# Order of the background work in a selective-scan layer: when y is written back, how the first image is normed, how the last image is finished

## Chip, cores and metric

The kernel runs on one core of a Trainium2 chip. It is one program that computes four layers one after the other. The metric is device time in microseconds (us); the time of a kernel is the median of several runs. The engines are TensorE (PE in the profile), VectorE (DVE), ScalarE (ACT), GpSimd (POOL) and SyncE (SP, which here issues DMAs only). Each engine runs its own instructions strictly in order.

## The reference, cut to what matters

The input x is 8 images of 64 channels of 64 x 64 points. Layer 0 holds the whole change; its middle part is this (C = 64, DI = 128, N = 16, four scan directions):

```python
def _selective_scan(xs, dts, A, Bs, Cs, D):     # per direction k, channel d, state n
    def step(h, inp):
        u_t, dt_t, B_t, C_t = inp
        h = h * exp(dt_t[..., None] * A) + dt_t[..., None] * B_t[:, :, None, :] * u_t[..., None]
        return h, einsum('bkcn,bkn->bkc', h, C_t)
    ...
    return ys + D * xs

def _ss2d(x, ...):                              # x is already layer-normed over the channels
    xz = einsum('bhwc,dc->bhwd', x, in_proj_w) + in_proj_b
    xi, z = split(xz, 2)
    xc = silu(dwconv3(xi, conv_w, conv_b))      # 3 x 3, per channel
    xs = [rows of xc, columns of xc, rows reversed, columns reversed]
    dts, Bs, Cs = split(einsum('bkdl,kcd->bkcl', xs, xproj_w), [R, R + N])
    dts = softplus(einsum('bkrl,kdr->bkdl', dts, dtproj_w) + dtproj_b)
    out_y = _selective_scan(xs, dts, A, Bs, Cs, Ds)
    y = sum of the four directions, each put back into the order of the image
    y = ln(y, outnorm_g, outnorm_b) * silu(z)
    return einsum('bhwd,cd->bhwc', y, outproj_w) + outproj_b

xh = x + _ss2d(ln(x, ln1_g, ln1_b), ...)
return xh + _safm(channel_ln(xh), ...)
```

What follows (`_safm`, a layer with channel and spatial attention, one with an inner optimisation, one with attention) is the same before and after the change. It starts by reading `xh`, two images at a time.

## The kernel before, in words

`scan_layer` (L203 to L743) computes `xh`. An image is held with its 128 inner channels on the partitions and its 4096 points along the free axis. Points are cut twice: into 8 *blocks* of 512 (`BK`[...]) for everything around the scan, and into 4 *chunks* of 1024 (`CH`) for the scan itself.

**Steps and units.** A *step* is one direction k on one chunk c; an image has 16 steps (L643: directions in the order 0, 2, 1, 3, that is rows, rows reversed, columns, columns reversed; reversed directions take the chunks from the last to the first). A step has 16 *units*, one for each state n. Eight images give 128 steps and 2048 units. A unit n (`unit`, L585) does this:

- VectorE multiplies B, broadcast to all partitions (`bt`), by `du` = dt * u, into PSUM (`bdu`, L594). For n = 3 and 8 (`BY_POOL`) GpSimd does this product ahead of time and in place (`product`, L583), from a copy of the same numbers in SBUF (`dus`).
- VectorE runs the scan h = a * h + bdu along the 1024 points (L598).
- ScalarE copies the last column of h to `state`, from which the next chunk starts (L602).
- GpSimd multiplies the broadcast C (`ct`) by h, in place (L607). The multiplies of the units before n = 3 and n = 8 are held back by one unit, so that GpSimd does unit 3's own before unit 2's, and 8's before 7's.

Two units later `sum_up` (L621) has TensorE add the product into the PSUM tile `yps` by a matmul with the identity (L636). The tile begins, at n = 0 of a step, with the skip term (direction 0, weight `skipd`, source u) or with the y of the directions before (identity, source y; both L631). After n = 15 it is complete, and `empty` (L612) has ScalarE copy it to `y` (L616). There is one buffer of `yps`: the next step's L631 waits for that copy. `empty` is called at the head of each `sum_up`.

**What a unit needs and when it is issued.** The loop in L706 to L734 issues, around `unit(ctl, n)`: the load of `bt` for unit n + 3 and of `ct` for unit n + 1 (`load`, L566; on SP's queue, from a DRAM scratch `bc`; 4 buffers of `bt`, 5 of `ct`, so that a load waits on the queue until a buffer is free, and what is behind it on the queue waits too); `decay` for unit n + 2, on ScalarE (a = exp(A_n dt), L575, 3 buffers); `product` for n + 2. Past n = 15 these are those of the next step. The next step's `du` is copied by ScalarE into PSUM inside unit 15, between its product and its scan (`place_input`, L550), since there is one buffer of `du`.

**The background.** Everything else is cut into *items*, pairs of a `make` (mostly a matmul into one of two PSUM banks, tag "mm") and a `use` (mostly an activation that empties it). `Background` (L165) keeps them in a queue. In each unit, `bg.before()` ahead of the unit's own work makes the next item, and `bg.after()` behind it issues the DMAs that the item before left (`later`), then the `use` of the previous unit's item. So there is one item in a unit. Items are:

- `project` (L476), for the next step, put at the head of the queue: B and C (`lower`, twice; ScalarE copies to `e`, then a DMA to `bc`), dt before softplus (`step_size`, twice), softplus in three parts (Abs, Exp; Ln, Relu on ScalarE; a sum on GpSimd, `soft3`), and for columns one copy that turns u (`turn`). `soft3` and `step_input` (the `dus` product on GpSimd) are issued behind units 8 and 11, behind unit 13 in the first image's first four steps.
- `before` (L352), for the next image: 8 loads of x, `norm_items` (L271), 8 `project_in` into the padded image `pad`, 8 `gate` (z = Silu, stored to DRAM `zd`), 8 `convolve` (nine taps by nine matmuls with diagonal matrices, L405, in four items of 3, 2, 2 and 2 taps, in the first image in two of 5 and 4; then Silu into `u`).
- `after` (L427), for the image before: `norm_items` on y, product with z on GpSimd (`multiply`), `project_out` with the residual, store to `xh`.

`norm_items` is the layer norm for all 8 blocks: `centre` (subtract the mean by a matmul, square), `variance` (a matmul that gives a row, `vrow`, stored to DRAM), `fetch` (all variances back as 128 x 32), `root`, `invert`, store, `back` (1/std as rows), `apply` per block (spread by a matmul, multiply on VectorE, scale and offset on ScalarE).

**The ends.** In the first image there is no image before it to hide its `before`: `start(0)` and a `bg.drain()` run its loads, norm, projections and the first two convolutions ahead of step 0 (L685 to L693); convolutions 2s and 2s + 1 for s = 1 to 3 are put in front of step s's own items and so are done in step s - 1, and the gates follow in step 4. Before the last step of an image the queue is emptied (the `while bg.queue` ahead of `prepare(b + 1, 0)`). After the last step of the last image come the last sums, `empty`, and `after(7)` with nothing beside it. Then the next layer's first load, x (L1154), waits for `xh` of images 0 and 1 and its place in SP's queue, and its norm begins with L136.

## Time and profile before

The median is 13172.89 us of 3 runs (13163.58 to 13174.3). The profiled execution took 13181.03 us; its span, from the first instruction to the last, is 13179.2 us.

| stretch, us from the span's start | what runs | DVE busy | PE busy | ACT busy | POOL busy | PE clock granted |
|---|---|---|---|---|---|---|
| 0 to 123 | ahead of the first scan | 13.57 | 99.06 | 45.65 | 9.12 | 1.00 |
| 123 to 7723 | the 128 steps | 7162.75 | 6059.21 | 4790.90 | 6050.11 | .91 |
| 7723 to 7805 | after the last scan, until the next layer's first matmul on its x | 8.21 | 65.60 | 28.01 | 22.41 | .65 |
| 7805 to 13179 | the three other layers and the rest of layer 0 | 3797.89 | 4903.18 | 2867.00 | 694.68 | .94 |

How to read the lines shown later. A *group* line names line, engine, operation, output <- inputs, shape and count, then the total busy time and the mean of one in ns, then the idle time of the engine just before these instructions and what ended most of it. A line of the view by source line gives min/median/max in ns, then the stretch of the span in which they lie. A line of the *waits* gives the engine and the line that waited, what it waited for, the total, the number of times and the longest, in us. A *timeline* line gives start and duration in us, engine and line, and in square brackets how long the engine had been idle before it and what it waited for; SPq is the DMA queue's issue. Idle time of an engine that is not the one that sets the end costs nothing. The matmuls' ends are modelled.

### The profile page before, as it was taken

To read this page: it belongs to the slowest core of one execution; us is meant where nothing else is said; L and a number is where in the kernel's file an instruction comes from. 1 tells how busy PE (TensorE), PEld (TensorE's weight loads), DVE (VectorE), ACT (ScalarE), POOL (GpSimd) and SP (SyncE) were. 2 spreads that over 40 slices of the span, in tenths; PEclk is the share of its full clock that TensorE was granted. 3 is DMA by queue.
4 is the path that set the end of the run, shared out by engine and by line. 5 is a ranking of instruction groups with operands and counts; after the bars stand their busy time and mean duration, and the time that the engine had idled before them with its cause. 6 is when DMAs were issued, how large, how long until landed. Compare 5 with 4: busy or idle time off the path is not lost. (4 is left out here: it accounts for less than half of the span.)

```text
span 13179.2 us, 115966 instructions
## 1 busy us (share of the span) xinstructions
PE 11127.1 (84%) x36395; PEld 4134.4 (31%) x36395; DVE 10982.4 (83%) x7626; ACT 7731.6 (59%) x10048; POOL 6776.3 (51%) x3126
## 2 busy tenths in 40 slices
PE   8787887788888878877877779999997778999999
PEld 2232232232232232322322223323324554333332
DVE  6999999999999999999999958686686786666666
ACT  5675666665666766665765536455464674544544
POOL 5778878778778778778778840000002772000000
PEclk9898999898999999999998879999998788999999
DMA  5888888888888888888888840000001010000000
GB/s 196 289 281 291 302 290 294 293 286 301 292 285 306 288 291 300 290 285 303 288 287 299 289 158 9 23 13 17 17 6 63 29 37 25 5 17 17 5 11 6
DMA packets 684840, 2333.69 MB, mean 177 GB/s; under 512 B 96784, under 2 KB 97456, under 8 KB 681648
## 3 DMA queue, kind: packets, MB, share of 16 engines
q1 hardware_dynamic: 684208, 2326.13, 51.1%
q8 instruction: 290, 4.75, 0.1%
q14 instruction: 342, 2.80, 0.1%
HBM read 2240.69 MB, written 76.28 MB: 176 GB/s over the span
## 5 line engine op out<-in xcount | busy, mean ns | idle before, releaser
L607 POOL TENSOR_TENSOR ct<-ct,h 128x1024 f32<-128x1024 f32 x2048 | 4820.7, 2369 | 1546.7 <-DVE h L598 779.5
L636 PE MATMUL yps<-ct,ident 128*128 128x512 f32 x8192 | 4157.3, 641 | 542.2 <-POOL ct L607 540.9
L598 DVE TENSOR_TENSOR_SCAN h<-a,state,bdu 128x1024 f32<-128x1024 f32 x1344 | 3153.9, 2347 | 193.1 <-POOL ct L607 15.1
L892 DVE TENSOR_TENSOR sum<-sum,ex 128x1024 f32<-128x1024 f32 x1920 | 2348.0, 1223 | 767.0 <-ACT ex L885 653.6
L885 ACT ACTIVATE ex<-sc 128x1024 f32<-128x1024 f32 x2048 | 1985.1, 1021 | 1526.5 <-PE sc L880 1526.3
L636 PEld LDWEIGHTS yps<-ct,ident 128*128 128x128 f32 x8192 | 1573.6, 202 | 3084.1 <-issue 1893.4
L575 ACT ACTIVATE a<-dt,amat 128x1024 f32<-128x1024 f32 x2048 | 2337.2, 1142 | 22.7 <-POOL dt L528 19.5
L594 DVE TENSOR_TENSOR bdu<-bt,du 128x1024 f32<-128x1024 f32 x1792 | 2194.4, 1225 | 186.7 <-ACT du L554 123.8
L899 PE MATMUL av<-ex,v 128*64 128x512 f32 x8192 | 1985.9, 606 | 0.0
L602 ACT COPY state<-h 128x1 f32<-128x1 f32 x2048 | 381.4, 186 | 2251.4 <-DVE h L598 2247.6
L880 PE MATMUL sc<-q,k 16*128 16x512 f32 (+1 forms) x8192 | 1655.0, 628 | 5.0 <-ACT ex L885 4.4
L598 DVE TENSOR_TENSOR_SCAN h<-a,bdu 128x1024 f32<-128x1024 f32 x448 | 1024.5, 2287 | 65.7 <-ACT state L602 4.8
L899 PEld LDWEIGHTS av<-ex,v 128*64 128x64 f32 x8192 | 497.7, 136 | 1361.6 <-issue 1358.2
L880 PEld LDWEIGHTS sc<-q,k 16*128 16x128 f32 (+1 forms) x8192 | 562.5, 184 | 1078.4 <-ACT ex L885 744.3
L1197 POOL TENSOR_TENSOR gt<-gt,pad 128x1024 f32<-128x1024 f32 x16 | 34.9, 2181 | 1617.6 <-ACT gt L1196 1535.5
L631 PE MATMUL yps<-y,ident 128*128 128x512 f32 x384 | 344.7, 1039 | 386.3 <-ACT y L616 386.3
L583 POOL TENSOR_TENSOR bt<-bt,dus 128x1024 f32<-128x1024 f32 x256 | 603.1, 2356 | 5.2 <-DMA bt<-bc 4.7
L598 DVE TENSOR_TENSOR_SCAN h<-a,state,bt 128x1024 f32<-128x1024 f32 x192 | 566.3, 2950 | 20.5 <-POOL bt L583 19.0
L405 PE MATMUL vps<-pad,convd 128*128 128x512 f32 x1152 | 535.4, 594 | 1.5 <-ACT z L390 1.5
L1570 DVE RECIPROCAL r<-e 128x512 f32<-128x512 f32 x128 | 420.7, 3323 | 0.0
L512 ACT ACTIVATE dt<-tps,dtb 128x512 f32<-128x512 f32 x256 | 175.1, 684 | 361.6 <-PE tps L505 361.6
L528 POOL TENSOR_TENSOR dt<-dt,e 128x1024 f32<-128x1024 f32 x128 | 300.9, 2351 | 111.0 <-ACT dt L525 111.0
(402 smaller groups left out, 10439.3 us busy)
## 6 DMA issues: line engine op xcount, KB each, us to landing
bt<-bc SPq DMA_DIRECT2D x2048, 512.0 KB
ct<-bc SPq DMA_DIRECT2D x2048, 512.0 KB
x<-x SPq DMA_DIRECT2D x12, 2048.0 KB
bc<-e SPq DMA_DIRECT2D x256, 64.0 KB
zd<-z SPq DMA_DIRECT2D x64, 256.0 KB
z<-zd SPq DMA_DIRECT2D x64, 256.0 KB
x<-x SPq DMA_DIRECT2D x32, 512.0 KB
part<-x SPq DMA_DIRECT2D x128, 128.0 KB
```

What stands on the lines that cost most here:

```text
L405: nc.tensor.matmul(held[0].rearrange("p (r c) -> p r c", c=S), convd[:, t, :], pad[:, j * rows + dy : (j + 1) * rows + dy, dx : dx + S], s ...
L575: nc.scalar.activation(ctl["a", n], ctl["dt"], AF.Exp, scale=amat[:, ctl["k"], n : n + 1])
L583: nc.gpsimd.tensor_tensor(bt, bt, ctl["dus"], ALU.mult)
L594: nc.vector.tensor_tensor(z, bt, ctl["du"], ALU.mult)
L598: nc.vector.tensor_tensor_scan(h[:, flip], a[:, flip], z[:, flip], 0.0 if state is None else state[:, n : n + 1], ALU.mult, ALU.add,)
L607: nc.gpsimd.tensor_tensor(ct, ct, h, ALU.mult)
L636: nc.tensor.matmul(ctl["ps"][:, bass.ts(i, BK)], cm.ident, ct[:, bass.ts(i, BK)], start=False, stop=(n == N - 1),)
L880: nc.tensor.matmul(sc[:, e, :], k[r : r + d, bass.ts(j, 128)], qs[i][r : r + d, :], start=True, stop=True,)
L885: nc.scalar.activation(ex, sc, AF.Exp)
L892: nc.vector.tensor_tensor(sums[i], sums[i], ex, ALU.add)
L899: nc.tensor.matmul(avs[i][r, :], v[:, j, r], ex[:, e, :], start=(j == 0), stop=(j == TQ - 1))
L1570: nc.vector.reciprocal(r[n][s], e[n][:, s])
```

## The change

**y is written back sooner.** `empty` leaves `sum_up` and stands at the head of each unit, in front of the background item and the unit's own work. In unit 13 no background item is started (`bg.before(n == N - 3)`), though the `use` of unit 12's still runs. In unit 15 the next step's `decay` is issued behind `unit` (and so behind `place_input`) and not in front of it.

**The first image is normed in three parts.** `norm_items` takes the blocks it is for, and scales its DRAM row and its small tiles to them. For image 0 it is made three times, for blocks 0 to 2, 3 and 4, 5 to 7 (`FIRST`), each followed by the projections of these blocks. The first part and convolutions 0 and 1 stay ahead of step 0; the second goes into step 0, the third into step 1, each in front of the two convolutions that were there before; in step 2 are the last two convolutions. In these three steps (`early`) each unit has three background items, the two more behind it. `pad` is filled to the end two steps later than before.

**The last image ends with rows and is finished beside its last steps.** The directions of image 7 come in the order 1, 3, 0, 2. Direction 2 goes through the chunks from the last to the first, so that after each of its steps two blocks of y are final. `after` takes the blocks it is for; in steps 13, 14 and 15 of image 7 (`late`) it is added behind unit 4 for the two blocks of the step before, and these steps have two items a unit. After the last step only blocks 0 and 1 are left. Because y no longer begins with direction 0, the skip term goes with the first four steps of an image (`new_y`), whichever direction these are. `load` of x and z in `after` becomes one item ahead of the last two `apply`.

For images 1 to 6 the items are the same as before but for one more item in each `after` (the `load`).

```diff
@@ -181,7 +181,7 @@
         self.late.append(do)
 
-    def before(self):
+    def before(self, skip=False):
         self.now = None
-        if self.queue:
+        if self.queue and not skip:
             make, use = self.queue.popleft()
             self.now = (use, make() if make else None)
@@ -269,10 +269,10 @@
             return psum.tile([128, BK], F32, name=name, tag="mm")
 
-        def norm_items(src, dst, p, consts, g, b):
-
+        def norm_items(src, p, consts, g, b, blocks=range(NBK)):
 
             cen, avg = consts
-            var = dr.tile([L], F32, name="vard", tag="vard")
-            rs = dr.tile([L], F32, name="rsd", tag="rsd")
+            j0, nb = blocks[0], len(blocks)
+            var = dr.tile([L], F32, name="vard", tag="vard")[: nb * BK]
+            rs = dr.tile([L], F32, name="rsd", tag="rsd")[: nb * BK]
             sq, sm = {}, {}
 
...
@@ -336,18 +336,21 @@
                 def use(ps):
                     nc.vector.tensor_tensor(src[:, blk], src[:, blk], ps[:p], ALU.mult)
-                    nc.scalar.activation(dst(j), src[:, blk], AF.Identity, bias=b, scale=g)
+                    nc.scalar.activation(src[:, blk], src[:, blk], AF.Identity, bias=b, scale=g)
 
                 return make, use
 
-            out = [centre(0), centre(1)]
-            for j in range(NBK):
+            none = (None, None)
+            out = [centre(j) for j in blocks[:2]]
+            for j in blocks:
                 out.append(variance(j))
-                if j + 2 < NBK:
+                if j + 2 - j0 < nb:
                     out.append(centre(j + 2))
-            none = (None, None)
             out += [none, (None, fetch), none, (None, root), (None, invert), none, (None, back)]
-            out += [none] + [apply(j) for j in range(NBK)]
+            out += [none] + [apply(j) for j in blocks]
             return out
 
+
+        FIRST = (range(3), range(3, 5), range(5, 8))
+
         def before(b):
 
@@ -420,10 +423,11 @@
                 ]
 
-            items = [(None, load(j)) for j in range(NBK)]
-            items += norm_items(xn, lambda j: xn[:, bass.ts(j, BK)], C, ln1, ln1_g, ln1_b)
-            items += [project_in(j) for j in range(NBK)]
+            items = [[(None, load(j)) for j in range(NBK)]]
+            for blocks in (FIRST if b == 0 else (range(NBK),)):
+                items.append(norm_items(xn, C, ln1, ln1_g, ln1_b, blocks))
+                items[-1] += [project_in(j) for j in blocks]
             return u, zd, items, [gate(j) for j in range(NBK)], [convolve(j) for j in range(NBK)]
 
-        def after(b, y, zd):
+        def after(b, y, zd, blocks=range(NBK)):
 
             xf = x_in[b].rearrange("c h w -> c (h w)")
@@ -454,16 +458,19 @@
                     nc.scalar.activation(xo[:C], po[:C], AF.Identity, bias=outb)
                     bg.later(lambda: nc.sync.dma_start(xh[b][:, bass.ts(j, BK)], xo[:C]))
-                    if j + 3 < NBK:
+                    if j + 3 in blocks:
                         load(j + 3)
-                    if j + 2 < NBK:
+                    if j + 2 in blocks:
                         multiply(j + 2)
 
                 return make, use
 
-            items = norm_items(y, lambda j: y[:, bass.ts(j, BK)], DI, lno, on_g, on_b)
-            items[-4] = (items[-4][0], lambda ps, use=items[-4][1]: (use(ps), load(0), load(1)))
-            items[-1] = (items[-1][0], lambda ps, use=items[-1][1]: (use(ps), load(2)))
-            items += [(None, lambda _: (multiply(0), multiply(1))), (None, None)]
-            return items + [project_out(j) for j in range(NBK)]
+            def begin(_):
+                for j in blocks[:2]:
+                    multiply(j)
+
+            items = norm_items(y, DI, lno, on_g, on_b, blocks)
+            items.insert(-2, (None, lambda _: [load(j) for j in blocks[:3]]))
+            items += [(None, begin), (None, None)]
+            return items + [project_out(j) for j in blocks]
 
         def ordered(t, k, c):
@@ -622,9 +629,8 @@
 
 
-            empty()
             ctl, n, ct = pending.popleft()
             if n == 0:
                 ctl["ps"] = psy.tile([DI, CH], F32, name="yps", tag="yps")
-                wt, src = (skipd, ctl["u"]) if ctl["k"] == 0 else (cm.ident, ctl["y"])
+                wt, src = (skipd, ctl["u"]) if ctl["new_y"] else (cm.ident, ctl["y"])
                 so, half = ordered(src, ctl["k"], ctl["c"]), BK // S
                 for i in range(CH // BK):
@@ -641,8 +647,13 @@
                 full.append(ctl)
 
-        steps = []
-        for k in (0, 2, 1, 3):
-            cs = range(NCH) if k < 2 else range(NCH - 1, -1, -1)
-            steps += [(k, c, i) for i, c in enumerate(cs)]
+        def steps(b):
+
+
+            out = []
+            for k in (0, 2, 1, 3) if b < NB - 1 else (1, 3, 0, 2):
+                cs = range(NCH) if k < 2 else range(NCH - 1, -1, -1)
+                out += [(k, c, i) for i, c in enumerate(cs)]
+            return out
+
         images = {}
 
@@ -660,5 +671,5 @@
             return dict(
                 k=k, c=c, u=u, y=y, dt=dt, bc=bc, ut=ut, soft3=soft3, new=new, state=None,
-                first=(i == 0),
+                first=(i == 0), new_y=(s < NCH),
             )
 
@@ -671,9 +682,9 @@
             y = io.tile([DI, L], F32, name="y", tag="y")
             images[b] = (u, zd, y)
-            bg.add(items)
+            bg.add(items[0] + items[1])
             if b == 0:
-                for s in range(1, NCH):
-                    later[s] = convs[2 * s] + convs[2 * s + 1]
                 bg.add(convs[0] + convs[1])
+                for s in range(1, NCH):
+                    later[s] = sum(items[s + 1 : s + 2], []) + convs[2 * s] + convs[2 * s + 1]
                 later[NCH] = gates
             else:
@@ -697,11 +708,12 @@
             place_input(ctl)
             for b in range(NB):
-                for s in range(len(steps)):
-                    if s + 1 < len(steps):
+                for s in range(4 * NCH):
+
+
+                    early, late = b == 0 and s + 1 < NCH, b == NB - 1 and s > 3 * NCH
+                    if s + 1 < 4 * NCH:
                         nxt = prepare(b, s + 1)
                     else:
-                        while bg.queue:
-                            bg.before()
-                            bg.after()
+                        bg.drain()
                         nxt = prepare(b + 1, 0)
 
@@ -713,21 +725,32 @@
 
                     for n in range(N):
-                        bg.before()
+                        empty()
+
+                        bg.before(n == N - 3)
                         ahead(load, n + 3, 0)
                         ahead(load, n + 1, 1)
-                        ahead(decay, n + 2)
+                        if n < N - 1:
+                            ahead(decay, n + 2)
                         ahead(product, n + 2)
                         unit(ctl, n, nxt)
+                        if n == N - 1:
+                            ahead(decay, n + 2)
                         if len(pending) + len(ready) > LAG:
                             sum_up()
                         bg.after()
+                        for _ in range(2 * early + late):
+                            bg.before()
+                            bg.after()
 
-                        if n == (13 if b == 0 and s < NCH else 8) and nxt:
+                        if n == (13 if early else 8) and nxt:
                             nxt["soft3"]()
-                        if n == (13 if b == 0 and s < NCH else 11) and nxt:
+                        if n == (13 if early else 11) and nxt:
                             step_input(nxt)
 
                         if s == 0 and n == LAG + 2 and b > 0:
                             bg.add(after(b - 1, images[b - 1][2], images.pop(b - 1)[1]))
+                        if late and n == LAG + 2:
+                            c = 4 * NCH - s
+                            bg.add(after(b, images[b][2], images[b][1], range(2 * c, 2 * c + 2)))
                         if s == (1 if b else NCH) and n == 0 and b + 1 < NB:
                             bg.add(later.pop(NCH, []))
@@ -740,5 +763,5 @@
                 sum_up()
             empty()
-            bg.add(after(NB - 1, images[NB - 1][2], images[NB - 1][1]))
+            bg.add(after(NB - 1, images[NB - 1][2], images[NB - 1][1], range(2)))
             bg.drain()
 
```

## The prediction, made before the changed kernel was run

> **What bounds the kernel.** I read the page first, then the wait totals, then the timeline of one step. VectorE is busy for 7162.75 of the 7600 us from the first scan (123.15) to the end of the last (7723.03), so it bounds the scan layer. A unit is a product (1.23 us) and a scan (2.35 us); fourteen of these at 3.745 us and two units without product (2.3 us) make 57.0 us a step. The VectorE timeline has 59.4 us on average (7600/128) and 56.9 to 57.1 in the best steps: about 300 us are loss.
>
> The page (count | busy, mean ns | idle before, what ended it), then the scans of `bt` in the view of their line (min/median/max ns):
>
> ```profile
> L594 DVE TENSOR_TENSOR bdu<-bt,du 128x1024 f32<-128x1024 f32 x1792 | 2194.4, 1225 | 186.7 <-ACT du L554 123.8
> ...
> L598 DVE TENSOR_TENSOR_SCAN h<-a,state,bt 128x1024 f32<-128x1024 f32 x192 | 566.3, 2950 | 20.5 <-POOL bt L583 19.0
> ```
> ```profile
> L598 DVE TENSOR_TENSOR_SCAN h<-a,state,bt x192: 2323/2328/4465, 189.7 to 7693.0; 128x1024 f32<-128x1024 f32 x192
> L598 DVE TENSOR_TENSOR_SCAN h<-a,bt x64: 2265/2269/4449, 132.6 to 7517.8; 128x1024 f32<-128x1024 f32 x64
> ```
>
> Four losses. Scans of `bt` (units 3 and 8) stretch to 4.46 us where a GpSimd product runs beside them: 192 x (2.950-2.328) + 64 x (3.105-2.269) = 173 us, nearly all in unit 8. VectorE waits for `du` at a step's first unit: 123.8 less 48.1 before the very first, 76 us, and 9 more of the same that the view names after DMAs. It waits 37 us for GpSimd's `bt` and 17 for its `ct`.
>
> Waits from 600 to 7000 us (total, times, longest), then the timeline (start, duration) of the last step, whose unit 0 scans at 7666.17, show where most of it begins:
>
> ```profile
> POOL ct L607 <- DMA ct<-bc: 481.4, 230, 5.4
> PE yps L631 <- ACT y L616: 383.1, 93, 7.2
> ```
> ```profile
> 7667.28 1.98 PE L636 MATMUL yps<-ct,ident 128*128 128x512 f32 x4 [1.74 <-POOL ct L607]
> ...
> 7676.10 1.89 ACT L616 COPY y<-yps 128x1024 f32<-128x1024 f32 x1
> 7678.05 3.78 PE L631 MATMUL yps<-y,ident 128*128 128x512 f32 x4 [8.78 <-ACT y L616]
> ...
> 7683.84 0.32 SPq L571 DMA_DIRECT2D ct<-bc  x1
> ...
> 7687.86 2.36 POOL L607 TENSOR_TENSOR ct<-ct,h 128x1024 f32<-128x1024 f32 x1 [2.50 <-DMA ct<-bc]
> ...
> 7690.17 2.36 POOL L583 TENSOR_TENSOR bt<-bt,dus 128x1024 f32<-128x1024 f32 x1
> ...
> 7692.48 2.35 POOL L607 TENSOR_TENSOR ct<-ct,h 128x1024 f32<-128x1024 f32 x1
> 7692.96 4.02 DVE L598 TENSOR_TENSOR_SCAN h<-a,state,bt 128x1024 f32<-128x1024 f32 x1
> ```
>
> The old step's sums end at 7669.26. ScalarE has the copy of y behind unit 2's state copy and starts it at 7676.10. TensorE is idle until 7678.05; the first new sum ends at 7683.8; only then is a `ct` buffer free and its load issued. It lands 4.0 us later, 2.3 us after GpSimd had the h for it, and so the product of unit 6 (7692.48) meets unit 8's scan.
>
> **y sooner.** `empty()` now stands at the head of a unit: the copy comes behind unit 1's state copy (7672.26) and goes at 7672.35, 3.75 us earlier. Behind it on ScalarE are `decay` of unit 4 and unit 2's state copy; `decay` ends at 7672.35+1.89+1.15 = 7675.4, for a scan at 7679.5: hidden. The load goes at 7680.1 and lands at 7684.1, before the h. Unit 6's product then ends at 7692.7, 0.3 us before the scan: 4.02 becomes 2.33. It isn't so everywhere. In three steps of images 0 to 6 a half-done convolution holds one of the two PSUM banks, so that the second `lower` (in front of y's matmul on TensorE) waits for an `e` copy behind unit 2's state; 2 of the 3.75 us are won. Another step has eight 1.27 us gate products on GpSimd, 57 us with its own 47; another has the gates' table changes on ScalarE. I keep 63 of the 173 us and 34 of the 54: -130.
>
> `du`: at unit 15 the decay (1.15) now follows it, and since unit 13 starts no background item, unit 14's (a gate: 1.28+0.69+1.28 = 3.25) isn't in front. The commonest long wait, 5.09 us, loses 4.4. I keep 25 of 85: -60.
>
> The skipped slot has a price. Steps 0 to 14 of an image had 240 background slots for 228 items; now 225 for 229. What is left, a whole convolution block (nine taps), is drained in a burst ahead of step 15: 18 records at 0.44 us (12.29 for 28, below) = 7.9 from 0.6 before unit 0's scan, Silu 0.69, table 1.28, then decay of unit 2 (1.15), wanted 7.4 after it: 10.4-7.4 = 3 us, and 1 for the late sums behind it: 4 x 7 images = +28.
>
> Part: **-162**, bounds -32 (`du` alone) and -200.
>
> **First image.** Its start (start, duration):
>
> ```profile
> 108.34 12.29 PE L405 MATMUL vps<-pad,convd 128*128 128x512 f32 x28
> ...
> 123.15 2.29 DVE L598 TENSOR_TENSOR_SCAN h<-a,bdu 128x1024 f32<-128x1024 f32 x1
> ```
>
> Blocks 3 to 7 leave the part ahead of it: the last `vrow` ends at 33.3, not 51.7 (-18.4), and five applies and five projections at 1.71 us each go (-17.1): **-35.5**.
>
> They come back in steps 0 to 2 at three items a unit, and there each engine's order counts. Step 0, in us after scan 5: the first `pad` copy ends at 0.8 (it stands behind unit 5's state copy); TensorE then has 14 taps (12.3), one sum (1.8) and 4 taps (3.5); ScalarE stands at the second block's Silu (0.7), with a table load (1.28) and decay 9 (1.15) behind it: 21.5. VectorE wants that decay at 11.1: stall 10.4. Softplus (7.5 with its tables) is next in front of decay 11, and no lead is left: 4.9. The norm itself puts 1.9 us of work on VectorE and about 5 of waits: root for the variance's way out and back (2.2), two multiplies for `rstd`'s (3.1). Step 0: +22. Step 1 likewise, two blocks of nine taps after scan 6: decay 10 is 1.7 late, decay 11 (behind both Silus and two `e` copies) 9.6, softplus 3.3, norm 4.5: +19. Step 2 has no norm: decay 3 is 2.4 late, decay 4 7.9, then 0.6 and 4.3: +15. Together **+56**. On SP three stores, fetches and returns, about 1.6 us of waiting each, get between the `ct` and `bt` loads; these have 3 units' lead, and where they are late VectorE is standing anyway. Bounds: 0 if ScalarE keeps its two units' lead, 70.
>
> A rule speaks against the change here: the Trainium skill, *ScalarE: Activation LUTs*, section What ACT_TABLE_LOAD costs, gives a switch 1.28 us plus 1.38 of drain. In the trace a load begins at 132.92, takes 1.28, and its activation starts at 134.22: no drain. Eleven switches on these paths would make it +71 by the rule; I take the row's +56.
>
> **Last image.** The tail (start, duration):
>
> ```profile
> 7727.58 1.87 ACT L616 COPY y<-yps 128x1024 f32<-128x1024 f32 x1 [4.32 <-PE yps L636]
> ...
> 7795.47 0.53 SPq L1154 DMA_DIRECT2D x<-xh  x1
> ...
> 7804.51 3.75 PE L136 MATMUL cps<-x,p_cen 128*128 128x512 f32 x4 [2.82 <-DVE p_cen L116]
> ```
>
> With two blocks the last `vrow` ends at 7735.8 instead of 7750.0, the second apply at 7748.4, GpSimd's last product at 7749.8 instead of 7794.5. The next layer's load of x follows at 7750.8; its 8.2 us then set the start, 7759 for 7804.5: **-45.5**, bounds -40 and -47. Six blocks move beside steps 13 to 15: on VectorE 2 x 0.69 + 0.53 = 1.9 us a step, and 1.8 of waits (a reciprocal right behind the root, with a table load 1.28 between); TensorE, GpSimd and the DMAs have no next image to serve there. 3 x 3.7 = **+11** (0 to 20). That passes swap places moves no work.
>
> **Sum**, against the profiled execution's own time, 13181 (span 13179.2): -162-35.5+56-45.5+11 = -176, 13,005. The median of the runs is 8 us lower: **12,997**.
>
> **Rivals.**
> - A (0.50): as worked out, 12,950 to 13,045.
> - B (0.25): ScalarE keeps its lead in steps 0 to 2. For it: the old step 0 held 18 taps too and took 56.8 us. Against: 14 of these had begun before its first scan. 50 less: 12,947; with y's full 200, 12,909.
> - C (0.19): the 0.3 us before unit 8's scan are lost, products still meet it, only `du` is won: -32 for -162, in all -46: 13,127. Against it: in steps 1 and 2 of image 0 the load went 14.8 us after unit 0's scan, and unit 8's took 2.3.
> - D (0.04), slower: y's copy, in front of decay 4, waits for the last sums. From 10.4 us after unit 0's scan each us later is one of VectorE's in 127 steps; 11.8 eats the gain (178), 12.5 gives 13,263. The timeline has them at 3.1 to 7.6, in one step of an image at 10.3.
> - The change does nothing (0.02).
>
> **Numbers.** Some 0.2% (26 us) is what a measurement tells from no change. A, B and most of C are faster: 0.92; same 0.04; slower 0.04. The range leaves out B's best end, the worse half of C, and D: 12,905 to 13,110.
>
> **What would show it.** Right: first scan near 88 us; y's copy 6 to 8 us into a step, not 9.9; `ct` waits below 200; `bt` scans at 2.5 us in the mean; `du` waits near 65 with the first; steps 0 to 2 at 79, 76 and 73 us; step 15 at 61; last scan to x load 28 us, not 72. Wrong: last sums late, `bt` scans still at 2.9, or steps 0 to 2 below 60.

## The result

The changed kernel takes 12,990.08 us (median of 4 runs, 12,976.09 to 13,005.49) against 13,173.59 us of the kernel before on the same chip: a ratio of 0.9862 (95% interval 0.9845 to 0.9879). The prediction was 12,997, with 12,905 to 13,110 as its range. The profiled execution's span is 12,993.6 us, 185.6 less than before; the sum of the prediction said 176 less.

A step is measured below from its unit 0's scan to the next step's. In microseconds, from the scans' starts in the traces:

| stretch | before | after | difference |
|---|---|---|---|
| start to first scan | 123.2 | 87.7 | -35.4 |
| image 0, steps 0 to 2 | 172.5 | 245.3 | +72.8 |
| image 0, steps 3 to 15 | 786.0 | 765.4 | -20.6 |
| images 1 to 6 | 5706.7 | 5550.8 | -155.9 |
| image 7, steps 0 to 12 | 759.7 | 743.5 | -16.2 |
| image 7, steps 13 to 15 | 175.0 | 183.6 | +8.6 |
| last scan to the next layer's first matmul on x | 81.5 | 39.1 | -42.4 |
| the rest | 5374.7 | 5378.1 | +3.4 |

The page of the changed kernel has these groups (count | busy, mean ns | idle before, what ended it); behind the edits the line numbers are 3 to 23 higher than before:

```profile
L601 DVE TENSOR_TENSOR bdu<-bt,du 128x1024 f32<-128x1024 f32 x1792 | 2194.9, 1225 | 101.4 <-ACT du L561 46.3
...
L605 DVE TENSOR_TENSOR_SCAN h<-a,state,bt 128x1024 f32<-128x1024 f32 x192 | 499.5, 2602 | 15.0 <-POOL bt L590 8.2
```

Of the 46.3 us for `du`, 40.1 lie before the very first product; 6.2 are left in the steps, of 85. The scans of `bt` fell from 2.95 to 2.60 us in the mean. The waits from 600 to 7000 us (total, times, longest), and one ordinary step (image 3, step 14, unit 0's scan at 3756.15; start, duration):

```profile
POOL ct L614 <- DMA ct<-bc: 194.2, 102, 6.7
PE yps L637 <- ACT y L623: 116.4, 78, 3.3
```
```profile
3763.42 1.91 ACT L623 COPY y<-yps 128x1024 f32<-128x1024 f32 x1
...
3765.38 3.68 PE L637 MATMUL yps<-y,ident 128*128 128x512 f32 x4 [3.31 <-ACT y L623]
...
3771.24 0.32 SPq L578 DMA_DIRECT2D ct<-bc  x1
...
3776.06 2.37 POOL L614 TENSOR_TENSOR ct<-ct,h 128x1024 f32<-128x1024 f32 x1 [0.71 <-DMA ct<-bc]
...
3778.37 2.38 POOL L590 TENSOR_TENSOR bt<-bt,dus 128x1024 f32<-128x1024 f32 x1
...
3780.69 2.38 POOL L614 TENSOR_TENSOR ct<-ct,h 128x1024 f32<-128x1024 f32 x1
3780.71 2.35 DVE L605 TENSOR_TENSOR_SCAN h<-a,state,bdu 128x1024 f32<-128x1024 f32 x1
...
3782.97 2.32 DVE L605 TENSOR_TENSOR_SCAN h<-a,state,bt 128x1024 f32<-128x1024 f32 x1
```

y is copied 7.3 us into the step, not 9.9; the load of `ct` goes at 15.1, not 17.7 (9.9 and 17.7 are those of the step that the prediction shows); and unit 6's product ends at 3783.1, as unit 8's scan begins, which takes 2.32 us. Over the 127 copies inside steps the median place went from 9.9 to 7.2 us.

The price is in the first image. VectorE's timeline in steps 0 and 1 (in brackets how long it had stood, and for what):

```profile
87.72 2.29 DVE L605 TENSOR_TENSOR_SCAN h<-a,bdu 128x1024 f32<-128x1024 f32 x1
...
102.77 0.17 DVE L315 TENSOR_SCALAR vsm<-vsm 128x8 f32<-128x8 f32 x1 [5.52 <-DMA vsm<-vard]
...
115.04 0.68 DVE L337 TENSOR_TENSOR xn<-xn,rps 64x512 f32<-64x512 f32 x1 [4.18 <-PE rps L333]
...
141.75 2.29 DVE L605 TENSOR_TENSOR_SCAN h<-a,bdu 128x1024 f32<-128x1024 f32 x1 [11.83 <-ACT state L609]
...
153.81 2.29 DVE L605 TENSOR_TENSOR_SCAN h<-a,bdu 128x1024 f32<-128x1024 f32 x1 [4.83 <-ACT a L582]
...
193.00 0.17 DVE L315 TENSOR_SCALAR vsm<-vsm 128x12 f32<-128x12 f32 x1 [7.77 <-DMA vsm<-vard]
...
241.79 2.35 DVE L605 TENSOR_TENSOR_SCAN h<-a,state,bdu 128x1024 f32<-128x1024 f32 x1 [9.53 <-ACT a L582]
```

Two kinds of stall stand here: scans behind ScalarE (11.83, 4.83, 9.53), and the norm's own small instructions behind their data (5.52, 4.18, 7.77). The two fetches that the adds at 102.77 and 193.00 wait for, on SP's queue:

```profile
97.39 0.37 SPq L312 DMA_DIRECT2D vsm<-vard  x1
...
191.43 0.34 SPq L312 DMA_DIRECT2D vsm<-vard  x1
```

The tail, last scan's end 7576.34:

```profile
7586.84 1.01 ACT L623 COPY y<-yps 128x1024 f32<-128x1024 f32 x1 [4.66 <-PE yps L642]
...
7606.73 0.32 SPq L1177 DMA_DIRECT2D x<-xh  x1
...
7615.45 3.75 PE L136 MATMUL cps<-x,p_cen 128*128 128x512 f32 x4 [4.08 <-DVE p_cen L116]
```

The next layer's load of x goes 30.4 us after the last scan; it was 72.4. y's last copy starts 10.5 us after the last scan, and before it was 4.6: the last sums now stand on TensorE behind a `project_out` of step 15's own background.

### The profile page after: what moved, and what is told of

Read it like the earlier page. It is cut to its first block, busy times and chain, and to the rows that moved or that the text cites. A ratio compares the mean times of both kernels' runs of the same rounds, so it can differ in the third digit from the quotient of the medians.

```text
span 12993.6 us, 115955 instructions
## 1 busy us (share of the span) xinstructions
PE 11161.9 (86%) x36395; PEld 4115.1 (32%) x36395; DVE 10881.6 (84%) x7636; ACT 7717.6 (59%) x10047; POOL 6754.4 (52%) x3126
## 5 line engine op out<-in xcount | busy, mean ns | idle before, releaser
L642 PE MATMUL yps<-ct,ident 128*128 128x512 f32 x8192 | 4233.9, 652 | 547.3 <-POOL ct L614 545.3
L601 DVE TENSOR_TENSOR bdu<-bt,du 128x1024 f32<-128x1024 f32 x1792 | 2194.9, 1225 | 101.4 <-ACT du L561 46.3
L605 DVE TENSOR_TENSOR_SCAN h<-a,bdu 128x1024 f32<-128x1024 f32 x448 | 1024.3, 2286 | 83.5 <-ACT state L609 16.7
L903 PEld LDWEIGHTS sc<-q,k 16*128 16x128 f32 (+1 forms) x8192 | 562.1, 184 | 1078.8 <-ACT ex L908 743.5
L605 DVE TENSOR_TENSOR_SCAN h<-a,state,bt 128x1024 f32<-128x1024 f32 x192 | 499.5, 2602 | 15.0 <-POOL bt L590 8.2
L637 PE MATMUL yps<-y,ident 128*128 128x512 f32 x384 | 301.7, 917 | 115.6 <-ACT y L623 115.5
L1596 POOL TENSOR_TENSOR r<-r,half 128x512 f32<-128x512 f32 x128 | 162.7, 1271 | 360.9 <-issue 188.0
```

The lines of the kernel that those rows point to most:

```text
L601: nc.vector.tensor_tensor(z, bt, ctl["du"], ALU.mult)
L605: nc.vector.tensor_tensor_scan(h[:, flip], a[:, flip], z[:, flip], 0.0 if state is None else state[:, n : n + 1], ALU.mult, ALU.add,)
L642: nc.tensor.matmul(ctl["ps"][:, bass.ts(i, BK)], cm.ident, ct[:, bass.ts(i, BK)], start=False, stop=(n == N - 1),)
L903: nc.tensor.matmul(sc[:, e, :], k[r : r + d, bass.ts(j, 128)], qs[i][r : r + d, :], start=True, stop=True,)
```

## The experiments

The theory to be tested: the three parts of the change are independent and of the sizes in the prediction. The rivals: the gain of the y part comes from another of its edits, or from another part; and the first image's stalls have another cause than the convolutions. The medians of the kernel before were 13,166 to 13,182 us from one set of runs to the next, so a time is to be read by its ratio, and the parts by the steps' lengths. These come from one trace of each kernel; in images 1 to 6 the eight kernels that have the same items there (changed, e2, e3, e7 to e11) lie between 5544 and 5555 us, so some 10 us there tell nothing:

| kernel | median us | ratio to before (95%) | first scan | steps 0-2 | images 1-6 | image 7, 13-15 | last scan to matmul |
|---|---|---|---|---|---|---|---|
| changed kernel | 12,990 | 0.9862 (.9845-.9879) | 87.7 | 245.3 | 5550.8 | 183.6 | 39.1 |
| e1 y part alone | 12,997 | 0.9873 (.9857-.9890) | 123.0 | 172.5 | 5571.1 | 168.5 | 80.4 |
| e2 without first part | 12,956 | 0.9841 (.9824-.9857) | 122.3 | 172.1 | 5555.0 | 189.4 | 35.4 |
| e3 normed ahead, three items | 12,982 | 0.9861 (.9844-.9877) | 123.7 | 199.6 | 5552.4 | 187.8 | 38.5 |
| e4 y at the head only | 13,011 | 0.9884 (.9868-.9901) | 122.2 | 172.0 | 5577.3 | 168.4 | 81.6 |
| e5 head and moved decay | 13,010 | 0.9869 (.9852-.9885) | 123.1 | 171.9 | 5586.5 | 168.4 | 81.6 |
| e6 e2 with unit 13's item | 12,993 | 0.9858 (.9841-.9872) | 122.4 | 172.6 | 5584.9 | 194.3 | 39.1 |
| e7 two items, steps 0 and 2 | 12,975 | 0.9843 (.9827-.9860) | 87.9 | 233.0 | 5547.2 | 190.0 | 37.6 |
| e8 two parts | 12,951 | 0.9824 (.9808-.9841) | 101.5 | 190.8 | 5551.4 | 189.6 | 37.1 |
| e9 without first and last part | 12,976 | 0.9856 (.9839-.9872) | 123.7 | 172.0 | 5548.3 | 168.5 | 80.1 |
| e10 gaps in the norm | 12,973 | 0.9850 (.9834-.9866) | 88.0 | 228.9 | 5550.4 | 191.8 | 37.4 |
| e11 two parts, gaps | 12,958 | 0.9843 (.9826-.9859) | 101.7 | 202.5 | 5544.1 | 189.0 | 37.9 |
| e12 e8, second item in step 14 | 12,945 | 0.9820 (.9806-.9833) | 101.2 | 189.5 | 5544.0 | 186.0 | 39.8 |

### e1: the y part alone

On the kernel before:

```diff
         def sum_up():
-            empty()
...
                     for n in range(N):
-                        bg.before()
+                        empty()
+
+                        bg.before(n == N - 3)
...
-                        ahead(decay, n + 2)
+                        if n < N - 1:
+                            ahead(decay, n + 2)
                         ahead(product, n + 2)
                         unit(ctl, n, nxt)
+                        if n == N - 1:
+                            ahead(decay, n + 2)
```

> The kernel before with the y part alone (empty at the head of a unit, unit 13 without background item, decay behind unit 15; first and last image as before). The prediction's term was -162, which gives 13,011. The steps of the changed kernel that hold nothing but this part say more: images 1 to 6 went from 951 to 925 us each (-156), steps 3 to 15 of image 0 lost 21, steps 0 to 12 of image 7 lost 16. If the three parts are independent this kernel takes 12,970 to 12,985, its bt scans of unit 8 take 2.65 us in the mean, and the other two parts together cost the changed kernel something. If part of that gain came from the other parts (the first image's convolutions or z products out of the way), it stays at 13,010 or above.

12,997 us. The 128 steps take 7417 us, 183 less than before's 7600: neither 193 less, as independent parts would give, nor 162. Unit 8's scans take 2.82 us in the mean, the changed kernel's 2.65. Images 1 to 6 are 20 us longer than in the changed kernel, in their steps 12 to 14. Something else in the change helps them; e9 finds it.

### e2: the first image as before

On the changed kernel:

```diff
-        FIRST = (range(3), range(3, 5), range(5, 8))
+        FIRST = (range(8),)
...
-                        for _ in range(2 * early + late):
+                        for _ in range(late):
```

> The changed kernel with the first image normed in one piece ahead of step 0 and one item a unit in steps 0 to 2, as before. The prediction had this part at -35.5 and +56, so undoing it gives 12,990 - 20 = 12,970. The traces show -35.4 at the start and +72.8 in steps 0 to 2, which gives 12,950 to 12,955, faster than both kernels, with steps 0 to 2 at 56 to 58 us. Rival: if the stalls of steps 0 to 2 come from y's copy or the skipped slot meeting the convolutions, they stay, steps 0 to 2 are above 65 and the time is at or above 12,990.

12,956 us, as the traces had said. Steps 0 to 2 are back at 172.1 us, and the first scan at 122.3. So the first part brings -34.6 at the start and +73.2 in the steps: by these stretches it makes the kernel some 38 us slower (the two ratios differ by 0.2%, and their intervals overlap), and the rival (y's copy or the empty slot as the cause of those stalls) is out.

### e3: all normed ahead, but three items a unit

```diff
-        FIRST = (range(3), range(3, 5), range(5, 8))
+        FIRST = (range(8),)
```

> The changed kernel with all blocks of the first image normed ahead of step 0 (as before), but still three items a unit in steps 0 to 2, so that only the convolutions and the next step's projections come in a burst there. Theory of the prediction (ScalarE and TensorE lose their lead behind a convolution burst): the stalls of units 9 and 11 in step 0 (16.7 us), of units 10 to 13 in step 1 (15.3) and of units 4 to 6 in step 2 (11.9) remain, only the norm's waits and work go (about 13 us in step 0, 19 in step 1): steps 0 to 2 at about 72, 72 and 69, time 12,985 to 13,000. Rival (the norm's items and their waits on VectorE are what costs): steps 0 to 2 at 57 to 60, time 12,955.

Steps 0 to 2 take 63.1, 68.3 and 68.3 us: between the two theories. The convolutions at three items a unit cost 27 us of the 73 by themselves; with the norm beside them come another 46. Step 2, which has no norm in either kernel, is the same (68.9 and 68.3). In step 0 the convolutions alone stall scans by 2.2 and 4.3 us, not 16.7; here they come at the head of the step, not in its middle behind the norm.

### e4: only y's copy at the head of a unit

The first two changes of e1's diff, with `bg.before()` as it was.

> The kernel before with nothing but y's copy moved to the head of a unit: unit 13 keeps its item and unit 15's decay stays in front. The prediction had -130 for the copy, -60 for du and +28 for the skipped slot: 13,173 - 130 = 13,043, with du waits at 76 us as before and the scan of unit 8 at about 2.9 us. From the traces (scans of bt 173 to about 80 us of stretch, waits for bt and ct 54 to 14) the copy alone is worth -133 or so: 13,040. Rival: the skipped slot in unit 13 is what frees ScalarE for the last sums and y, and the copy alone leaves unit 8 at 3.3 us or more: above 13,090.

13,011 us. The steps take 7427.8 us, so the copy's place is worth 172 us of the 183, not 130: unit 8's scans are at 2.57 us, better than in any other kernel here, and the waits for `bt` and `ct` fell from 54 to 14 us. The waits for `du` stay, 69 us in the steps.

### e5: the same with the moved decay

> The kernel before with y's copy at the head and unit 15's decay behind du's copy, but with a background item in unit 13. It stands between e4 (neither; 13,011, du waits 69 us) and e1 (both; 12,997, du waits 7 us, but unit 8's scans at 2.82 instead of 2.57 us, steps 14 and 15 of an image 1.5 to 2.5 us longer). The prediction's reading of the commonest long wait for du, 5.09 us, was 1.15 for the decay and 3.25 for unit 14's item: then the moved decay alone takes 23 x 1.15 = 26 us of the 69, without the skipped slot's price: 12,985 to 12,990, faster than e1. Rival 1: the decay alone frees du altogether: 12,950. Rival 2: the skipped slot does all of it, the decay nothing: 13,005 to 13,015.

The three kernels' lines for `du` (e4, e5, e1; idle before, and of it for `du`, of which 47 to 48 us lie before the very first product in each):

```profile
L594 DVE TENSOR_TENSOR bdu<-bt,du 128x1024 f32<-128x1024 f32 x1792 | 2194.6, 1225 | 177.7 <-ACT du L554 116.5
```
```profile
L594 DVE TENSOR_TENSOR bdu<-bt,du 128x1024 f32<-128x1024 f32 x1792 | 2194.9, 1225 | 141.5 <-ACT du L554 87.4
```
```profile
L594 DVE TENSOR_TENSOR bdu<-bt,du 128x1024 f32<-128x1024 f32 x1792 | 2194.4, 1225 | 109.8 <-ACT du L554 54.8
```

The decay alone takes 30 us of the 69 (26 were expected) and the empty slot 33 more. But the steps are no shorter for it: 7432.7 us against e4's 7427.8. What `du` no longer waits, the stretched scans (+15 us), scans that wait for a late `state` copy of ScalarE (+12) and waits for `bt` (+10) take. The slot then brings 7417.1. So both edits for `du` together net 11 us here, not the 32 (-60 and +28) of the prediction, and 11 us are little more than the scatter between kernels.

### e6: e2 with an item in unit 13

```diff
-                        bg.before(n == N - 3)
+                        bg.before()
```

> e2 (first image as before; 12,956) with a background item in unit 13. The last convolution block need not be drained ahead of step 15 then: ScalarE's late state copies in steps 15 (30 us in e2) go, and unit 8's scans fall from 2.62 to about 2.57 us (-6), but du waits come back by 40 us (69 less 26 for the moved decay), so about the same, 12,950 to 12,970. If the skipped slot was worth more than it costs, 12,975 or more; if less, 12,945 or less.

12,993 us, the expectation missed on the slow side: the empty slot is worth more than it costs. That rests on the steps' lengths, for the ratios of e6 and e2 overlap in their intervals. Images 1 to 6 are 30 us longer, with `du` waiting 37 us again; step 15 is 56.8 us instead of 61.0, as expected. In e5 and e1, without the `load` item, the same slot brought 16 us.

### e7: two items a unit in steps 0 and 2

```diff
-                        for _ in range(2 * early + late):
+                        for _ in range(early + (early and s == 1) + late):
```

> The changed kernel with two background items a unit instead of three in steps 0 and 2 of the first image (step 1 keeps three, its items need them). Theory 1 (the convolution burst stalls ScalarE): spread over more units, step 0 falls from 85.4 to about 76 and step 2 from 68.9 to about 62, step 1 stays at 91: 12,974. Theory 2 (the norm's waits on VectorE are the larger term, as e3 hints for step 0: 22 of 28.6 us): step 0 stays at 81 or above, step 2, which has no norm, falls to 60 to 64: 12,979 to 12,984. If the burst isn't the cause at all, all three steps stay.

76.4, 90.1 and 66.5 us: step 0 as the first theory has it, step 1 unchanged, step 2 less than hoped. The pace of the items is a cause; it isn't all of it. Nor does the run tell the two theories apart: in step 0 the stalls behind the convolutions fell from 16.7 to 8.6 us and the norm's waits from 11.1 to 1.8, while `du` at the next step's head waits 7.0 us instead of 1.0.

### e8: two parts, the second beside step 0

```diff
-        FIRST = (range(3), range(3, 5), range(5, 8))
+        FIRST = (range(5), range(5, 8))
...
                 for s in range(1, NCH):
-                    later[s] = sum(items[s + 1 : s + 2], []) + convs[2 * s] + convs[2 * s + 1]
+                    later[s] = convs[2 * s] + convs[2 * s + 1]
+                later["norm"] = items[2]
...
                         nxt = prepare(b, s + 1)
+                        bg.add(later.pop("norm", []))
...
-                        for _ in range(2 * early + late):
+                        for _ in range((early and s == 0) + late):
```

> The changed kernel with the first image normed in two parts: blocks 0 to 4 ahead of step 0, blocks 5 to 7 behind step 0's own convolutions and projections, two items a unit in step 0, one in steps 1 and 2. Start: three vrow of 3.7 us and three applies and projections of 1.71 us each less, -21 against e2 (first scan near 101). Step 0: three multiplies on VectorE and the norm's waits, 12 us by the prediction's sizes, so 12,947, faster than e2. Rival: the norm of three blocks costs in step 0 what it cost in step 1 of the changed kernel (91.0 less e3's 68.3, 22.7 us): 12,958, no gain over e2.

12,951 us. The first scan comes at 101.5, 20.8 us sooner than in e2, and steps 0 to 2 return 18.7 of them. The steps say 2 us of gain over e2 and the ratios 0.9824 and 0.9841 overlap in their intervals: no gain that is shown.

### e9: neither first nor last part

e2 with the order of directions, the steps 13 to 15 and the tail of before; only the y part is left, and the `load` that became an item of its own in `after`. Two small things more differ from e1: the drain ahead of step 15 also runs the last convolution's Silu, which e1 leaves to unit 0, and `soft3` and `step_input` of image 0's step 3 stand behind units 8 and 11.

```diff
-            for k in (0, 2, 1, 3) if b < NB - 1 else (1, 3, 0, 2):
+            for k in (0, 2, 1, 3):
...
-                    early, late = b == 0 and s + 1 < NCH, b == NB - 1 and s > 3 * NCH
+                    early, late = b == 0 and s + 1 < NCH, False
...
-            bg.add(after(NB - 1, images[NB - 1][2], images[NB - 1][1], range(2)))
+            bg.add(after(NB - 1, images[NB - 1][2], images[NB - 1][1]))
```

> e2 without the last-image part: direction order 0, 2, 1, 3 in all images, one item a unit in steps 13 to 15, all eight blocks finished behind the last step. Against e1 it differs only in one more item in each image's after (the load of x and z). Theory: the last part is worth -45 behind the last scan and +21 in steps 13 to 15 of image 7 (e2 against e1), so this kernel takes 24 us more than e2, 12,980 relative to the runs of before at 13,166, and the 17 us by which images 1 to 6 are shorter in e2 than in e1 come from the extra item, which shifts the items behind it by one unit: its 128 steps take 7,400 us, e1's 7,417, e2's 7,424. Rival: those 17 us come with the last part or by chance; then the steps take 7,417 as in e1 and the last part is worth 38 in all.

The 128 steps take 7396.6 us, 20.5 less than e1's, as expected. The gain lies in steps 12 to 14, ahead of the drain, so the one item more is the cause, and the timelines show how: image 3, step 14 (unit 0's scan at 3728.32 in e1, 3715.28 in e9; lines of e1, then of e9):

```profile
3736.72 1.91 ACT L616 COPY y<-yps 128x1024 f32<-128x1024 f32 x1 [1.02 <-PE yps L635]
...
3740.15 1.91 PE L487 MATMUL dps<-ut,wx 128*32 128x512 f32 x2 [3.48 <-ACT e L495]
...
3742.00 3.79 PE L630 MATMUL yps<-y,ident 128*128 128x512 f32 x4
```
```profile
3720.16 1.04 PE L494 MATMUL dps<-ut,wx 128*32 128x512 f32 x2 [0.17 <-ACT u L417]
...
3722.56 1.91 ACT L623 COPY y<-yps 128x1024 f32<-128x1024 f32 x1
...
3724.52 3.78 PE L637 MATMUL yps<-y,ident 128*128 128x512 f32 x4 [3.32 <-ACT y L623]
```

In e1 the second `lower` stands on TensorE in front of y's matmul and waits for the `e` copy that frees its bank, because a convolution begun in the step before holds the other: y's matmul starts 13.7 us into the step. In e9 the items behind the extra one come a unit later, the step before ends with a whole convolution, whose Silu (L417) has just freed the bank, and y's matmul starts at 9.2. The same holds in steps 12 to 14 of all images from 1 to 6: 12.1 to 13.7 us in e1, 9.0 to 9.3 in e9 but for one of 10.6. These steps fall from 58.7 to 56.8 us in the mean; step 15 rises from 58.7 to 60.5, where 18 records of a convolution are now left for the drain and not 12 to 14 (the Silu that moved into the drain is a rival there that no run separates).

Against e2 this kernel gives the last part: -44.7 behind the last scan, +20.9 in steps 13 to 15. The changed kernel's own steps 13 to 15 are 15.1 us above e9's.

### e10: gaps in the norm

On the changed kernel:

```diff
-            out += [none, (None, fetch), none, (None, root), (None, invert), none, (None, back)]
-            out += [none] + [apply(j) for j in blocks]
+            gap = [none] * (4 if p == C and j0 > 0 else 0)
+            out += [none, (None, fetch), none] + gap
+            out += [(None, root), (None, invert), none, (None, back)]
+            out += gap + [none] + [apply(j) for j in blocks]
```

> The changed kernel with empty items in the parts of the first image's norm that run beside steps 0 and 1: four ahead of root, four ahead of the first apply. Nothing else moves, the number of items a unit stays three. Theory: the norm's waits on VectorE (11.1 us in step 0, 16.4 in step 1) are there because three items a unit leave fetch to root 0.7 of a unit where one item a unit leaves two; with eight gaps they fall to 2 to 4 us a step: step 0 at 77, step 1 at 79, step 2 as it was at 69, time 12,990 - 20 = 12,970. Rival 1: the waits only change places with convolution stalls that the norm's waits had covered: steps 0 and 1 lose less than 5 us each, 12,982 or more. Rival 2: the convolution burst comes later in the step and runs into softplus and du: a longer wait for du at the head of the next step.

75.8, 84.7 and 68.4 us, 16.4 less in all, 12,973 us (the ratio's interval overlaps the changed kernel's; the steps' lengths decide). All waits of VectorE over 2 us in step 0:

```profile
133.38 2.29 DVE L607 TENSOR_TENSOR_SCAN h<-a,bdu 128x1024 f32<-128x1024 f32 x1 [4.46 <-ACT a L584]
...
143.74 2.29 DVE L607 TENSOR_TENSOR_SCAN h<-a,bdu 128x1024 f32<-128x1024 f32 x1 [6.81 <-ACT state L611]
...
155.13 2.29 DVE L607 TENSOR_TENSOR_SCAN h<-a,bdu 128x1024 f32<-128x1024 f32 x1 [4.16 <-ACT a L584]
```

The norm's waits are gone from step 0 (11.1 us before), and 3.6 us are left in step 1 of 16.4: they were there because three items a unit bring `root` and `apply` up before their data. The scans' stalls behind the convolutions stay in step 0 (15.4 us for 16.7) and grow in step 1 (18.2 for 15.3, and 3.1 at unit 4): there, the first rival holds for half, though step 1 loses 6.3 us and not less than 5. The second doesn't show: `du` at the next step's head waits 1.1 to 1.3 us instead of 0.9 to 1.0.

### e11: two parts with gaps and a slower start

e8 with e10's gaps and

```diff
-                        for _ in range((early and s == 0) + late):
+                        for _ in range(2 * (early and s == 0 and n > 3) + late):
```

> e8 (blocks 5 to 7 normed in step 0) with the same gaps in the norm, one item a unit in units 0 to 3 of step 0 (the convolutions at the old pace) and three from unit 4 on. e8 lost 13 us in step 0 (69.8 for 56.8), 3.8 of them behind the convolutions and 5 in the norm's waits, and 5.5 in step 1. If pace and gaps are the causes, step 0 falls to 61 to 64: 6 to 9 us below e8. If three items a unit cost as such (late sums, DMAs in bunches), it stays at 68 or above.

Step 0 takes 75.0 us, a miss: the convolutions are still followed by stalls (2.5, 4.3, 2.8 us) and the waits move on into step 1 (7.6 us at its unit 4, 69.4 in all). Three items a unit cost more than the gaps save, as the expectation's other case has it (68 or above).

### e12: a second item late in step 14

On e8:

```diff
-                        for _ in range((early and s == 0) + late):
+                        for _ in range((early and s == 0) + late + (b < NB - 1 and s == 14 and n in (7, 9, 11, 12, 14))):
```

> e8 with a second background item in units 7, 9, 11, 12 and 14 of step 14 of images 0 to 6, so that the last convolution block is made there and nothing is left to drain ahead of step 15. Theory of the prediction (the burst of nine taps, its Silu and its tables stand in front of unit 2's decay): step 15 falls from 61.4 us to 57, as in the kernels that have an item in unit 13 (56.8), and step 14 rises by at most 1.5 us (56.9 now), since TensorE and ScalarE have one unit more for each part: 7 x 3 to 7 x 4 = -20 to -30, a ratio to before of 0.980 to 0.981. Rival 1: the taps cost the same wherever they are made two items a unit: step 14 rises by what step 15 loses, no gain. Rival 2: step 15 is long because unit 13's empty slot moves dt and softplus, not for the burst: step 15 stays at 60 or more.

The burst ahead of step 15 in the changed kernel (image 3, unit 0's scan at 3813.13), and what follows it on ScalarE:

```profile
3810.53 7.89 PE L408 MATMUL vps<-pad,convd 128*128 128x512 f32 x18
...
3818.46 0.69 ACT L417 ACTIVATE u<-vps,convb 128x512 f32<-128x512 f32 x1 [3.82 <-PE vps L408]
3819.16 1.28 ACT L582 ACT_TABLE_LOAD   x1
3820.46 1.15 ACT L582 ACTIVATE a<-dt,amat 128x1024 f32<-128x1024 f32 x1
```

With e12, 8 to 9 of the 18 records are left at that place in images 1 to 6: five more items weren't enough to empty the queue. Step 15 takes 60.1 us instead of 61.4, its stalls 14.3 us over seven images instead of 22.3, and step 14 57.3 instead of 56.9. So half the burst takes away about a third of the stalls, and unit 8's scans there stay stretched, 3.0 to 4.4 us in six of seven images. The full gain wasn't reached, and at 60.1 us the second rival's own sign (60 or more) is met. What still comes late is the end of step 14's sums on TensorE: 9.1 to 12.2 us into step 15 in images 1 to 6, 11.1 to 12.3 in e8, but 3.1 to 6.3 in e6, which has an item in unit 13 and no burst. No kernel here has the burst without the empty slot, or the slot without a burst, so how much of step 15 is the burst's stays open. At 12,945 us (ratio 0.9820, 0.9806 to 0.9833) this is the fastest kernel of the study, 0.4% below the changed kernel by the ratios. e2 has half of that from leaving the three-part norm out; the intervals of e2, e8 and e12 overlap, so the rest isn't shown by the times.

## Why the prediction came out right

The time came out within 7 us, rival A's case. The paths were the right ones; that the sum is so near is luck, because errors in three terms (41, 17 and 4 to 10 us) cancelled in part. Term by term, sizes from the steps' lengths:

| term | predicted | measured | from |
|---|---|---|---|
| y sooner | -162 | -183, and -20 for the item | e1, e9 |
| first image, start | -35.5 | -34.6 | e2 to changed |
| first image, steps 0 to 2 | +56 | +73 | e2 to changed |
| last image, tail | -45.5 | -42 to -46 | changed, e2 |
| last image, steps 13 to 15 | +11 | +15 to +21 | e9 to changed, to e2 |

**y sooner.** The chain that was followed in the timeline is the right one, link by link, and e4 shows that the copy's place carries most of it (172 us). Sizes: of the stretched scans the prediction left 63 us and the changed kernel has 74 of 173; of the waits for `bt` and `ct` it left 34, there are 14; of those for `du` 25, there are 6. The waits for late `state` copies outside steps 0 to 2, the price of the empty slot, went from 6 to 28 us; +28 was the estimate, and the burst has the 18 records that it named, at the place that it named (e12). What failed is one sentence: that in three steps of images 0 to 6 a half-done convolution holds a bank. This holds in e1, where it costs 20 us, but in the changed kernel only in image 0 (y's matmul starts at 12.4 to 13.9 us in its steps 12 to 14, at 9.2 to 9.3 in the same steps of images 1 to 6 but for one of 10.6). The prediction counted the one item that `load` adds, as a slot, and didn't ask where it puts the convolution against the step's end.

**First image, start.** First scan 87.72 where 88 was said; both components were right. (What the prediction calls the end of the last `vrow`, 33.3 and 51.7, is where that copy starts, 33.26 and 51.73; the difference is the same.)

**First image, steps.** The stalls behind the convolutions were predicted at 15.3, 14.6 and 15.2 us and came to 16.7, 15.3 and 11.9: 43.9 for 45.1. The order on the engines was also as worked out (TensorE, then ScalarE, of step 0 of the changed kernel):

```profile
121.15 12.18 PE L408 MATMUL vps<-pad,convd 128*128 128x512 f32 x28
...
134.88 3.60 PE L408 MATMUL vps<-pad,convd 128*128 128x512 f32 x8
```
```profile
138.52 0.69 ACT L417 ACTIVATE u<-vps,convb 128x512 f32<-128x512 f32 x1 [8.76 <-PE vps L408]
139.22 1.28 ACT L582 ACT_TABLE_LOAD   x1
140.52 1.15 ACT L582 ACTIVATE a<-dt,amat 128x1024 f32<-128x1024 f32 x1
```

14 taps, a sum, 4 taps, Silu, table, decay. (e3 adds a caution: without the norm ahead of them the same convolutions cost 27 us, so the 44 aren't theirs alone.) The step that was mis-sized is the norm's waits: "about 5 of waits" for step 0, "norm 4.5" for step 1, which by its sum is work and waits together. The waits are 11.1 and 16.4, the work 1.7 and 2.4. Root was given 2.2 us for the variance's way; in step 0 it waits 5.5 for a fetch issued at its start, in step 1 7.8 for a fetch that SP issues only 6.2 us into the wait, behind the last `vrow` copy and its store. The prediction's sizes are like those of the drained start of the kernel before, where nothing is beside it (there the fetch takes 1.7 us, and `rstd`'s way 3.1), and it counted them from the place where VectorE comes to it, not from where the chain before it has got. e10 confirms the cause: with four empty items in front of each, 27.5 us of waits become 3.6.

**The rule on table loads.** The line at 139.22 shows it once more: the load starts as the Silu ends, takes 1.28 us, and the activation starts 1.30 us after the load's start. There is no drain of 1.38 us, which the Trainium skill adds (*ScalarE: Activation LUTs*, What ACT_TABLE_LOAD costs). The sum by the rule, +71, lies near the measured +73, but for another reason: the excess over +56 is in the norm's waits, which the trace puts down to fetches and to the `rps` matmuls and not to a table load, and the convolution stalls with their tables were sized right by the row.

**Last image.** The tail came within 3 us in its size, by two errors: y's last copy starts 6 us later than was reckoned, behind TensorE's late sums, and the chain behind it is 3 us shorter. In steps 13 to 15 of e2 the waits are 7.0 us (5.4 predicted), but VectorE's work is 10.2 instead of 5.7, since a tiny add takes 1.3 to 2.3 us there (below), and 4.7 us are stretched scans, which the prediction left out.

**The rivals.** B (ScalarE keeps its lead) is wrong for every step. C (products still meet unit 8's scans) is right for 34 of 128 steps, where the scan takes over 2.6 us; before it were 96. D (y's copy waits for late sums) shows in few steps: in images 1 to 6 the sums end 9.7 us into a step or sooner, but at 11.0 to 11.7 in step 15, after the burst; in image 0 they end at 12.9 and 15.4 in steps 1 and 2, and at 14.0 in step 15. That the first part of the change is a loss by itself followed from the prediction's own terms (+20) and is +38.

**The other signs.** The mean scan of `bt` was to be 2.5 us and is 2.60; the waits for `du`, with the first, 65 and are 46; steps 0 to 2 79, 76 and 73 us and are 85.4, 91.0 and 68.9, so that only step 2, without a norm, came out shorter than said; the load of x 28 us after the last scan and is 30.4. The waits for `ct`, below 200, and step 15, 61 us, came as said.

**What stays open.** Why the moved decay without the empty slot gives back all that it saves (e5) was read only from the sums of waits. Which of pace and place stalls the scans after the convolutions in e11 was not separated, nor what of step 15's length is the burst's and what the empty slot's (e12).

## What to carry to other kernels

When an in-order engine frees a buffer, follow what the next transfer in that buffer's chain collides with: a copy off the path, placed some 3 us sooner, was worth 1.2% by itself (e4), and the scans that it shortened are on another engine than the copy. A background queue is a clock: one item more or less shifts all behind it against the steps (20 us), so after an edit compare where the long items fall, not how many there are. Before moving start-up work beside the main loop, count for each of its small instructions on the bounding engine how long the data takes from the item before it, at the new pace of items; here 35 us won at the start cost 73 in the loop.

## What the runs showed of the hardware

An add of 128x8 elements on VectorE takes 0.17 us alone and 2.31 us beside a GpSimd product; it ends when the product ends (e2, image 7, step 15):

```profile
7517.88 4.65 POOL L614 TENSOR_TENSOR ct<-ct,h 128x1024 f32<-128x1024 f32 x2
...
7520.25 2.31 DVE L315 TENSOR_SCALAR vsm<-vsm 128x8 f32<-128x8 f32 x1 [1.21 <-DMA vsm<-vard]
```

The product in flight ends at 7522.53, the add at 7522.56. The other adds of this size that start beside a GpSimd product, in image 7 of all kernels with the last part, end 0.03 to 0.06 us after a product too. The prediction had looked for this only in scans, with two inputs in SBUF; the add has one, and a constant. The Trainium skill, *SBUF — State Buffer*, section Who interferes with whom, names instructions of VectorE in a mode that uses both ports for one input (`tensor_scalar` can be in one) beside those with two inputs, and says that whichever comes second waits for the whole instruction of the first. The trace agrees in that the add ends with the product; whether it ran in such a mode the trace doesn't tell. So an instruction of 0.17 us cost up to 2.3 us of VectorE, in each of the three last steps of e2 (2.00, 1.30 and 2.31 us).
